# A third place for the convolution's shares, its matrices moved one transfer per step, and a reordered last unit

## The chip, the cores and the metric

The kernel runs on one core of one Trainium2 chip. The metric is the device time of one execution in microseconds. TensorE (PE) multiplies matrices, VectorE (DVE) and ScalarE (ACT) work element by element, GpSimd (POOL) issues some small transfers and SyncE (SP) issues nearly all large ones.

## What is computed

Two attention layers over x of shape (4, 256, 64, 64), float32 throughout, each as `x = x + layer(groupnorm(x))`:

```
# layer 0: queries 1x1, keys and values by a strided 2x2 convolution, 8 heads of 32 channels
q = einsum('oc,bchw->bohw', Wq, x)            # 4096 queries per image
k = conv(x, Wk, stride 2); v = conv(x, Wv, stride 2)      # 1024 keys per image
attn = softmax((q.k + q.(rel_h + rel_w)) * 32**-0.5); out = attn.v
# layer 1: qkv 1x1, attention inside 4 areas of 1024 tokens, a 7x7 depthwise convolution of v, 1x1 projection
out = softmax(q.k * 32**-0.5).v               # per area
out = out + dwconv7x7(v_full, w_pe) + b_pe
return conv1x1(out, w_proj) + b_proj
```

## The kernel before

**Units and steps.** A block is one layer on one image: `BLOCKS` holds layer 0 ("A") of the four images, then layer 1 ("B") of the four. A block has 16 units, so there are 128 units; a unit is a chunk of 512 queries of four heads. A unit has eight steps, one for each 128 keys. In a step PE makes the scores of the step (`scores`, L263), ACT takes their exponentials (L267), and PE multiplies those of the step before with the values (`weighted`, L274). DVE adds the eight pairs of exponential tiles of a unit to one pair (`sum_up`, L813); when the sum is done, `divisors` (L283) multiplies it with ones, so that each row holds the sum of its exponentials, and `divide` (L287) divides by it. To divide, the sums go through DRAM into a narrow shape, `reciprocals` inverts them (L306), they come back spread over the rows (L308, L310), and `multiply` (L313) writes the result. The last unit of all does not take this way: its sums are copied by ACT (L292), inverted in full width by DVE (L295) and multiplied (L296).

**Order.** The order on every engine is the program's own (`manual_schedule`). `at(g, j, f)` plans f for step j of unit g (a larger j runs on into the following units). `task(parts, f)` puts matrix work that is not attention into a queue `side`, of which one part is done per step, two when more than 7 parts wait and three when more than 14 wait, one less in step 2; `soon_tasks` puts tasks in at the head of the queue. In a step the order is: scores, the functions that `soon` planned for it, `weighted`, the functions of `at`, then parts of the side queue. SP issues its transfers in program order too; it waits at one whose data or buffer is not ready, and all that follow wait behind it.

**PSUM.** `ps_pair` (three buffers of two banks) holds scores, divisors and, outside the 128 units, side products; `ps_side` (one buffer of one bank) holds side products within them.

**The depthwise convolution** of layer 1 is done by PE. `plan_values` computes the values of a chunk and stores them to DRAM (`vala`, L688, and `vals`, L696), after loading the chunk `hv` of the layer's input (L665). `plan_zeros` builds in DRAM, for each of 32 groups of eight channels, a band matrix of the 7x7 taps: `matrices(k)` loads eight shifted pieces into a tile `made` (L643) and stores it as `mats[k]` (L650). A *share* is one such group of one image: `load_share` (L713) brings its matrix (`band`, L728, one transfer) and its value rows (`rows`, L731, four transfers). Both have two buffers. `convolve` (L739) is a task of two parts, one share each: after the matrix products of a share (L747) it calls `load_share(False)` for the next one not yet loaded, which takes the buffers that this share gives back. `plan_conv` plans the 16 tasks of an image; before the first of them it fills the buffers:

```
        for _ in range(2 if n == 0 else 0):
            at(0, when - 8, lambda: len(loaded) < 2 and load_share(True))
        at(0, when, lambda: task(2, convolve, b, n))
```

They start at units 36, 58, 75.5 and 93.5 and are planned 1.36, 1.06, 1.1 and 1.1 units apart. The result goes through `cout` (L758, L759) to DRAM. `load_rest` (L551) fetches it for a chunk as `cv`, `add_conv` (L573) adds attention and bias, `project` (two tasks per chunk, L157 for the products, L588 for bias and residual) makes the output, and L591 stores it.

**Layer 0's weights.** `wk0_sb` and `wv0_sb` are two constant tiles of 8 KB per partition; `make_k` and `make_v` of layer 0 (L359, L380) read them, for the last image near unit 46.

**The end.** After unit 127: the last two DVE additions, `divisors`, `divide`, `multiply` of unit 126, `add_conv` and `project` of chunk 7, then `sum_last` (L773) with the sums for a check of their size (L857 to L862), whose count each engine loads at the very end.

Of the kernel before, what the change touches and what calls it, by code (L numbers as in the profile page):

```python
# [9 lines left out]
FP = mybir.dt.float32  # L10
I32 = mybir.dt.int32
AF = mybir.ActivationFunctionType
ALU = mybir.AluOpType
AX = mybir.AxisListType

P = 128
# [39 lines left out]
def direct_path(  # L56
# [52 lines left out]
    for c in range(NCH):  # L109
        nc.sync.dma_start(first[c], xv[0][:, :, c * CH : (c + 1) * CH])  # L110
    wq0_sb = const.tile([P, CT, C], FP, name="wq0_sb")
    wk0_sb = const.tile([P, CT, 4, C], FP, name="wk0_sb")
    wv0_sb = const.tile([P, CT, 4, C], FP, name="wv0_sb")
    wqkv_sb = const.tile([P, CT, 3, C], FP, name="wqkv_sb")
    wp_sb = const.tile([P, CT, C], FP, name="wp_sb")
    nc.sync.dma_start(wk0_sb, wk0.rearrange("(t p) k o -> p t k o", p=P))
# [42 lines left out]
    def ps_pair(name):  # L159
        return psum.tile([P, 2, CH], FP, tag="s", name=name, bufs=3)  # L160
# [9 lines left out]
    def at(g, j, f):  # L170
        g, j = g + int(j // NKT), int(j % NKT)
        plan.setdefault((g, j), []).append(f)
# [103 lines left out]
                rhs=p[h // 2][:, h % 2, :], start=(j == 0), stop=(j == NKT - 1),  # L276
            )

    def divisors(g, p):

        dens[g] = ps_pair("den")[:, 0, :]
        for h in range(4):
            T.matmul(  # L283
                dens[g][HD * h : HD * h + HD, :], lhsT=ones, rhs=p[h // 2][:, h % 2, :], start=True, stop=True,
            )

    def divide(g, unit):  # L287

        den_sb = pool.tile([P, CH], FP, tag="den", name="den_sb", bufs=1)
        few = pool.tile([P, 2, CH // HD], FP, tag="few", name="few", bufs=2)  # L290
        rows = dram.tile([4, CH], FP, tag="rows", name=f"rows_{g}", bufs=4)
        S.copy(den_sb, dens.pop(g))  # L292
        if g == len(units) - 1:
            rb = pool.tile([P, CH], FP, tag="p", name="rb", bufs=10)
            V.reciprocal(rb, den_sb)  # L295
            V.tensor_mul(unit[4]()[:, unit[0], :], avs.pop(g), rb)  # L296
            spare.extend((den_sb, rb))
            return
        G.dma_start(rows, den_sb[0:P:HD, :])  # L299
        G.dma_start(few[:, 0, :], rows.rearrange("h (q n) -> (h q) n", n=CH // HD))  # L300
        made = {}

        def reciprocals():
            rb = made["rb"] = pool.tile([P, CH], FP, tag="rb", name="rb", bufs=1)
            recs = dram.tile([4, CH], FP, tag="recs", name=f"recs_{g}", bufs=4)
            V.reciprocal(few[:, 1, :], few[:, 0, :])  # L306
            V.tensor_reduce(sums[:, :, g], few, AX.X, ALU.add)  # L307
            G.dma_start(recs.rearrange("h (q n) -> (h q) n", n=CH // HD), few[:, 1, :])  # L308
            for h in range(4):
                G.dma_start(rb[HD * h : HD * h + HD, :], recs[h : h + 1, :].to_broadcast([HD, CH]))  # L310

        def multiply():
            V.tensor_mul(unit[4]()[:, unit[0], :], avs.pop(g), made["rb"])  # L313

        at(g + 1, 7, reciprocals)
        at(g + 2, 4, multiply)

    def att_of(key):
        if key not in atts:
# [146 lines left out]
    def plan_b(b, u):  # L466
# [84 lines left out]
        def load_rest(c):  # L551
            cv = chunk_tile(f"cv_{b}_{c}")
            for y in range(c * RC, (c + 1) * RC):
                n, r = y // TY, TY - 1 - y % TY
                for t in range(CT):
                    nc.sync.dma_start(  # L556
                        cv[:, t, :].rearrange("p (f r x) -> p r f x", f=TX, r=RC)[:, y - c * RC],
                        conv[b][t * P : (t + 1) * P, r * TX : (r + 1) * TX, n, :],
                    )
            if c == NCH - 1:  # L560
                load_residual(c)
            rest[c] = cv
# [1 line left out]
        def by_column(a):  # L564
            return a.rearrange("p (f q) -> p q f", f=TX)

        def add_conv(c):
            cv, att = rest[c], atts["B", b, c]
            if c < NCH - 1:
                load_residual(c)  # L570
            for t in range(CT):

                V.scalar_tensor_tensor(  # L573
                    by_column(cv[:, t, :]), by_column(cv[:, t, :]), bpe_sb[:, t : t + 1],
                    att[:, t, :].rearrange("p (q f) -> p q f", f=TX), ALU.add, ALU.add,
                )

        def project(c, to):
# [10 lines left out]
            if to == 1:  # L589
                rest.pop(c)  # L590
                nc.sync.dma_start(ov[b][:, :, c * CH : (c + 1) * CH], made_x.pop(c))  # L591

        for c in range(NCH):
            g, j = u + 2 * c + 3, 5
            at(*((g - 1, 5) if b < B - 1 or c < NCH - 1 else (g - 2, 2)), lambda c=c: load_rest(c))
            at(g, j, lambda c=c: add_conv(c))
            at(g, j + 2, lambda c=c: soon_tasks([(2, project, c, to) for to in range(CT)]))
        return [
# [15 lines left out]
    def plan_zeros(g):  # L614


        def zeros():
            width = vals[0][0].rearrange("f c x -> (f c x)").shape[0] // P
            zero = pool.tile([P, max(3 * width, BY * BX * C // P)], FP, tag="rows", name="zero", bufs=2)
            V.memset(zero, 0.0)  # L620
            flat = bands.rearrange("k y x c -> (k y x c)").rearrange("(p n) -> p n", p=P)
            nc.sync.dma_start(flat, zero[:, : flat.shape[1]])
            for b in range(B):
                for lo, hi in ((0, HALO), (HALO + HH, HH + 2 * HALO)):
                    nc.sync.dma_start(
                        vals[b][lo:hi].rearrange("r f c x -> (r f c x)").rearrange("(p n) -> p n", p=P),
                        zero[:, : (hi - lo) * width],
                    )

        def taps():  # L630
            tap = pool.tile([NTAP, C], FP, tag="cout", name="tap", bufs=2)
            nc.sync.dma_start(tap, wpe.rearrange("c k -> k c"))
            for n in range(7):
                nc.sync.dma_start(
                    bands[:, TY - 1 : TY + 6, TX + 5 - n, :].rearrange("k y c -> y k c"),
                    tap[n : n + 43 : 7, :].rearrange("y (k c) -> y k c", c=TC),
                )

        def matrices(k):
            band = pool.tile([NP, 2, TY, TX * TC], FP, tag="band", name=f"made_{k}", bufs=2)  # L640
            for dc in range(TX + 6):
                p = NP // 2 * (dc // 2 % 2) + dc % 2
                nc.sync.dma_start(  # L643
                    band[p : p + 2 * (TY + 6) - 1 : 2, dc // 4],
                    bass.AP(
                        tensor=bands.tensor, offset=bands.offset + (k * BY * BX + TX + 5 - dc) * TC,
                        ap=[[BX * TC, TY + 6], [BX * TC, TY], [1, TX * TC]],
                    ),
                )
            nc.sync.dma_start(mats[k], band)  # L650

        at(g, 0, zeros)
        at(g, 4, taps)
        for k in range(C // TC):
            at(g + 1, 6 * k, lambda k=k: matrices(k))

    stored = {}

# [54 lines left out]
    def load_share(must):  # L713

        if not shares:
            return
        b, k = shares[0]
        for c in range(NCH):
            if must:
                need(stored, (b, c))  # L720
            elif (b, c) not in stored:
                return
        shares.popleft()
        row, size = C * XT, TC * XT
        band = pool.tile([NP, 2, TY, TX * TC], FP, tag="band", name=f"band_{b}_{k}", bufs=2)
        xs = pool.tile([NP, 2, NY, TC, XT], FP, tag="rows", name=f"rows_{b}_{k}", bufs=2)
        loaded[b, k] = band, xs
        nc.sync.dma_start(band, mats[k])  # L728
        for a in range(4):
            p = NP // 2 * (a % 2)  # L730
            nc.sync.dma_start(  # L731
                xs[p : p + NP // 2, a // 2].rearrange("p y c x -> p y (c x)")[:, :, : size - 3],
                bass.AP(
                    tensor=vals[b].tensor, offset=vals[b].offset + k * size + a,
                    ap=[[row, NP // 2], [TY * TX * row, NY], [1, size - 3]],
                ),
            )
# [26 lines left out]

    def plan_conv(b, n, start):
        when = int(start * NKT)
        for _ in range(2 if n == 0 else 0):
            at(0, when - 8, lambda: len(loaded) < 2 and load_share(True))
        at(0, when, lambda: task(2, convolve, b, n))

    def sum_last():
        for n in range(2):
            V.tensor_reduce(sums[:, n, len(units) - 1 :], spare[n], AX.X, ALU.add)  # L773

    at(len(BLOCKS) * UNITS + 1, 6, sum_last)
    units = []
    for i, (layer, b) in enumerate(BLOCKS):
        u = i * UNITS
# [29 lines left out]

    def sum_up(g, j, ps):

        for i in range(2):
            if j:
                soon(1, lambda i=i: V.tensor_add(ps[0][i], ps[0][i], ps[j][i]))  # L813
        if j == NKT - 1:
            soon(3, lambda: divisors(g, ps[0]))
            soon(3, lambda: divide(g, units[g]))
# [643 lines left out]
```

## Time and profile before

| | us |
|---|---|
| median of three runs | 3265.79 (3263.93 to 3267.28) |
| the profiled execution, its own time | 3265.73 |
| its span, first to last instruction | 3264.0 |
| PE busy | 3181.3 |
| DVE, ACT busy | 2508.4, 2524.3 |
| mean granted clock of PE | 0.989 |
| moved by DMA | 421.5 MB |

"Busy" of PE counts matrix instructions from start to modelled end, so a slow clock counts as busy. "L747" is line 747 of the kernel. In a line of the order of work the columns are start, duration (both us), engine and line, operation, names of output and inputs, count; in brackets the idle time of the engine before it and what ended that. "SPq" is the queue of SP. A wait is put down to what came last.

### The profile page before, as it was taken

The page shows a single profiled execution, that of the slowest core. Times are in us where ns is not written, and L with a number is a line of the kernel's source. Part 1 is how long each engine was busy: PE and PEld are TensorE (multiplying, and loading weights), DVE is VectorE, ACT ScalarE, POOL GpSimd, SP SyncE. Part 2 cuts the span into 40 slices and gives each one's busy share as a digit, 9 for nine tenths or more (in the row PEclk, how much of TensorE's full clock was granted, in tenths as well). Part 3 has the DMA queues.
Part 4 walks back from the last instruction along what each step waited for, and adds up shares of the span by engine and source line. Part 5 has one row for each costly group of instructions (what it writes and reads, how often), then busy time and mean ns, then how long its engine had stood idle before and what let it go on. Part 6 is the DMA issues. An engine that isn't in the chain of part 4 may idle for free.

```text
span 3264.0 us, 75650 instructions
## 1 busy us (share of the span) xinstructions
PE 3181.3 (97%) x30754; PEld 963.2 (30%) x30754; DVE 2508.4 (77%) x2717; ACT 2524.3 (77%) x2993; POOL 493.6 (15%) x923
## 2 busy tenths in 40 slices
PE   7999999999999999999999899999999999999997
PEld 4233322233233333223222223232232333222221
DVE  3777896778877777778767577777787788788887
ACT  3888787787887778888867677777777777788775
POOL 0111121111211111111111111111111111111111
PEclk9999999999999999999999999999999999999998
DMA  5243434454444456677766666666554655523212
GB/s 179 44 109 78 109 89 93 96 125 108 114 114 132 122 153 154 173 174 174 187 168 151 164 155 165 174 154 170 135 156 124 156 157 152 135 68 81 65 47 57
DMA packets 648172, 421.50 MB, mean 129 GB/s; under 512 B 411756, under 2 KB 556620, under 8 KB 647816
## 3 DMA queue, kind: packets, MB, share of 16 engines
q1 hardware_dynamic: 619368, 380.11, 46.0%
q0 software_dynamic: 28448, 36.48, 4.6%
q8 instruction: 244, 4.00, 0.5%
q14 instruction: 112, 0.92, 0.1%
HBM read 318.32 MB, written 98.09 MB: 128 GB/s over the span
## 4 chain that ended last, share of the span: by engine, by line
PE 87%; DMA 6%; issue 2%; SPq 2%; DVE 1%; ACT 1%; POOL 0%; DVEq 0%; ACTq 0%; POOLq 0%
PE s L263 31%; PE av L274 27%; PE den L283 4%; DMA rows<-vals 4%; PE ops L157 3%; PE k0ps L157 3%; PE q0ps L157 3%; PE v0ps L157 3%; PE k1ps L157 3%; PE vals_ps L157 3%; PE conv_ps L747 3%; PE q1ps L157 3%; DVE p L813 1%; ACT p L267 1%; SPq L556 1%
## 5 line engine op out<-in xcount | busy, mean ns | idle before, releaser
L813 DVE TENSOR_TENSOR p<-p 128x1024 f32<-128x1024 f32 x1792 | 2111.2, 1220 | 543.6 <-ACT p L267 491.1
L267 ACT ACTIVATE p<-s 128x1024 f32<-128x1024 f32 x2048 | 2016.3, 1026 | 539.0 <-PE s L263 524.3
L263 PE MATMUL s<-q,k_A 32*128 32x512 f32 x4096 | 603.9, 640 | 6.9 <-ACT p L267 6.6
L263 PE MATMUL s<-q,k_B 32*128 32x512 f32 x4096 | 600.1, 646 | 0.3 <-ACT p L267 0.3
L274 PE MATMUL av<-p,v_B 128*32 128x512 f32 x4096 | 550.5, 608 | 0.0
L274 PE MATMUL av<-p,v_A 128*32 128x512 f32 x4096 | 549.7, 604 | 0.0
L310 POOL DMA_DIRECT2D rb<-recs x508 | 252.0, 501 | 451.5 <-DMA recs<-few 367.1
L263 PEld LDWEIGHTS s<-q,k_B 32*128 32x128 f32 x4096 | 166.3, 184 | 386.7 <-issue 297.0
L263 PEld LDWEIGHTS s<-q,k_A 32*128 32x128 f32 x4096 | 173.2, 183 | 338.0 <-issue 253.5
L308 POOL DMA_DIRECT2D recs<-few x127 | 70.0, 551 | 1284.8 <-DVE sums L307 1207.5
L274 PEld LDWEIGHTS av<-p,v_B 128*32 128x32 f32 x4096 | 87.9, 108 | 384.2 <-issue 340.5
L274 PEld LDWEIGHTS av<-p,v_A 128*32 128x32 f32 x4096 | 88.6, 108 | 381.3 <-issue 333.5
L747 PE MATMUL conv_ps<-rows,band 88*32 88x128 f32 x4096 | 139.2, 277 | 28.9 <-DMA rows<-vals 28.9
L747 PEld LDWEIGHTS conv_ps<-rows,band 88*32 88x32 f32 x4096 | 123.8, 139 | 100.6 <-issue 80.3
L157 PE MATMUL ops<-cv,wp_sb 128*32 128x512 f32 x1024 | 136.3, 612 | 9.9 <-issue 6.4
L300 POOL DMA_DIRECT2D few<-rows x127 | 72.3, 569 | 477.5 <-DMA rows<-den_sb 468.0
L283 PE MATMUL den<-p,ones 128*32 128x512 f32 x1024 | 138.7, 604 | 2.2 <-DVE p L813 2.2
L299 POOL DMA_DIRECT2D rows<-den_sb x127 | 74.4, 586 | 436.7 <-ACT den_sb L292 429.9
L157 PE MATMUL k0ps<-taps,wk_sb 128*32 128x256 f32 x2048 | 128.9, 383 | 3.0 <-ACT taps L245 3.0
L157 PE MATMUL q1ps<-h,wqkv_sb 128*32 128x512 f32 x1024 | 131.5, 592 | 0.0
L157 PE MATMUL vals_ps<-hv,wqkv_sb 128*32 128x512 f32 x1024 | 130.2, 594 | 0.0
L157 PE MATMUL k1ps<-h,wqkv_sb 128*32 128x512 f32 x1024 | 128.7, 592 | 0.2 <-ACT cout L758 0.2
(86 smaller groups left out, 1690.8 us busy)
## 6 DMA issues: line engine op xcount, KB each, us to landing
rows<-vals SPq DMA_DIRECT2D x512, 195.9 KB
rb<-recs POOLq DMA_DIRECT2D x508, 64.0 KB, 3.2
band<-mats SPq DMA_DIRECT2D x128, 176.0 KB
vala<-vout SPq DMA_DIRECT2D x128, 144.0 KB
vals<-vout SPq DMA_DIRECT2D x128, 144.0 KB
vc<-vala SPq DMA_DIRECT2D x64, 288.0 KB
hq<-in_x SPq DMA_DIRECT2D x32, 512.0 KB
xc<-in_x SPq DMA_DIRECT2D x32, 512.0 KB
```

The costliest lines, as they stand in the source:

```text
L157: T.matmul(out[cols, :], lhsT=lhsT[:, cols], rhs=rhs, start=start, stop=stop)
L263: T.matmul(pairs[h // 2][:, h % 2, :], lhsT=k[rows, unit[0], j * P : (j + 1) * P], rhs=q[rows, :], start=True, stop=True,)
L267: exps = [lambda i=i: S.activation(p[i], pairs[i], AF.Exp, scale=SCALE) for i in range(2)]
L274: T.matmul(av[HD * h : HD * h + HD, :], lhsT=v[:, j, unit[0] * P + HD * h : unit[0] * P + HD * h + HD], rhs=p[h // 2][:, h % 2, :], start= ...
L283: T.matmul(dens[g][HD * h : HD * h + HD, :], lhsT=ones, rhs=p[h // 2][:, h % 2, :], start=True, stop=True,)
L299: G.dma_start(rows, den_sb[0:P:HD, :])
L300: G.dma_start(few[:, 0, :], rows.rearrange("h (q n) -> (h q) n", n=CH // HD))
L308: G.dma_start(recs.rearrange("h (q n) -> (h q) n", n=CH // HD), few[:, 1, :])
L310: G.dma_start(rb[HD * h : HD * h + HD, :], recs[h : h + 1, :].to_broadcast([HD, CH]))
L556: nc.sync.dma_start(cv[:, t, :].rearrange("p (f r x) -> p r f x", f=TX, r=RC)[:, y - c * RC], conv[b][t * P : (t + 1) * P, r * TX : (r + 1 ...
L747: T.matmul(ps[HD * m : HD * m + HD, (2 * k + i) * size : (2 * k + i + 1) * size].rearrange("p (y x) -> p y x", y=NY), lhsT=band[:, half].r ...
L813: soon(1, lambda i=i: V.tensor_add(ps[0][i], ps[0][i], ps[j][i]))
```

## The change

It has four edits. (1) The two weight tiles of layer 0 become one tile of 16 KB, and from image 1 on every third share has its matrix and rows in that place; so three shares are loaded instead of two. (2) The nine transfers of a matrix are planned one per step (the store in the eighth step, with the last load), eight steps to a matrix instead of six. (3) The last unit's sum takes seven of eight tiles; its eighth is multiplied with ones by PE and accumulated. Its reciprocal reads PSUM without the copy. (4) The last chunk's addition and projection are written out half by half, in the order in which the two halves of its attention come; `reciprocals` and `multiply` of unit 126 are planned earlier; the output of the chunk leaves in two transfers.

```diff
-    wk0_sb = const.tile([P, CT, 4, C], FP, name="wk0_sb")
-    wv0_sb = const.tile([P, CT, 4, C], FP, name="wv0_sb")
+    wkv = const.tile([P, 2, CT, 4, C], FP, tag="wkv", name="wkv")
+    wk0_sb, wv0_sb = wkv[:, 0], wkv[:, 1]
...
-    def divisors(g, p):
+    def divisors(g, *ps):
         dens[g] = ps_pair("den")[:, 0, :]
+        for n, p in enumerate(ps):
+            for h in range(4):
+                T.matmul(... ones, rhs=p[h // 2][:, h % 2, :], start=(n == 0), stop=(n == len(ps) - 1))
...
     def divide(g, unit):
+        if g == len(units) - 1:
+            rb = pool.tile([P, CH], FP, tag="p", name="rb", bufs=10)
+            V.reciprocal(rb, dens[g])
+            V.tensor_mul(unit[4]()[:, unit[0], :], avs.pop(g), rb)
+            spare.extend((dens.pop(g), rb))
+            return
...
-        at(g + 1, 7, reciprocals)
-        at(g + 2, 4, multiply)
+        at(g + 1, 7 if g < len(units) - 2 else 4, reciprocals)
+        at(g + 2, 4 if g < len(units) - 2 else 0, multiply)
...
+        def project_last(c):
+            cv, xm, ps = rest[c], made_x[c], [ps_pair("ops")[:, 0, :] for _ in range(CT)]
+            for t in range(CT):
+                if t == CT - 1:
+                    divide(len(units) - 1, units[-1])
+                    add_conv(c, [t])
+                    for n in range(2):
+                        V.tensor_reduce(sums[:, n, len(units) - 1 :], spare[n], AX.X, ALU.add)
+                for to in range(CT):
+                    product(ps[to], lhsT=wp_sb[:, t, to * P : (to + 1) * P], rhs=cv[:, t, :],
+                        start=(t == 0), stop=(t == CT - 1))
+            for to in range(CT):
+                x_to = xm[:, to, :].rearrange("p (q f) -> p q f", f=TX)
+                V.scalar_tensor_tensor(x_to, by_column(ps[to]), bproj_sb[:, to : to + 1], x_to, ALU.add, ALU.add)
+                nc.sync.dma_start(ov[b][:, to, c * CH : (c + 1) * CH], xm[:, to, :])
...
+            if b == B - 1 and c == NCH - 1:
+                at(g - 2, 2, lambda c=c: load_rest(c))
+                at(g - 1, 1, lambda c=c: add_conv(c, [0]))
+                at(g - 1, 3, lambda c=c: project_last(c))
+                continue
...
         for k in range(C // TC):
-            at(g + 1, 6 * k, lambda k=k: matrices(k))
+            for n in range(TX + 6):
+                at(g + 1, 8 * k + n, lambda k=k, n=n: matrices(k, [n]))
...
-        band = pool.tile([NP, 2, TY, TX * TC], FP, tag="band", name=f"band_{b}_{k}", bufs=2)
-        xs = pool.tile([NP, 2, NY, TC, XT], FP, tag="rows", name=f"rows_{b}_{k}", bufs=2)
+        if b and (b * (C // TC) + k) % 3 == 2:
+            place = const.tile([P, 2 * CT * 4 * C], FP, tag="wkv", name=f"share_{b}_{k}")
+            n = 2 * NY * size
+            xs = place[:NP, :n].rearrange("p (h y c x) -> p h y c x", h=2, y=NY, c=TC)
+            band = place[:NP, n : n + 2 * TY * TX * TC].rearrange("p (h y m) -> p h y m", h=2, y=TY)
+        else:
+            band = pool.tile(... tag="band", bufs=2)
+            xs = pool.tile(... tag="rows", bufs=2)
...
-        for _ in range(2 if n == 0 else 0):
-            at(0, when - 8, lambda: len(loaded) < 2 and load_share(True))
+        room = 3 if b else 2
+        for _ in range(room if n == 0 else 0):
+            at(0, when - 8, lambda: len(loaded) < room and load_share(True))
...
     def sum_up(g, j, ps):
+        if j == NKT - 1 and g == len(units) - 1:
+            soon(2, lambda: divisors(g, ps[0], ps[j]))
+            return
```

`sum_last` and its place in the plan are gone; its two reductions stand in `project_last`.

More of the change, by code (lines that the diff above doesn't have):

```diff
@@ L277, in weighted @@
             )
-    def divisors(g, p):
+    def divisors(g, *ps):
         dens[g] = ps_pair("den")[:, 0, :]
[L282 to L285, printed above, removed]
-    def divide(g, unit):
+        for n, p in enumerate(ps):
+            for h in range(4):
+                T.matmul(
+                    dens[g][HD * h : HD * h + HD, :], lhsT=ones, rhs=p[h // 2][:, h % 2, :],
+                    start=(n == 0), stop=(n == len(ps) - 1),
+                )
+    def divide(g, unit):
+        if g == len(units) - 1:
[4 more added lines that the diff above has]
+            return
         den_sb = pool.tile([P, CH], FP, tag="den", name="den_sb", bufs=1)
@@ L292, in divide @@
         S.copy(den_sb, dens.pop(g))
[L293 to L298, printed above, removed]
         G.dma_start(rows, den_sb[0:P:HD, :])
@@ L565, in by_column, with add_conv @@
             return a.rearrange("p (f q) -> p q f", f=TX)
-        def add_conv(c):
+        def add_conv(c, ts=range(CT)):
             cv, att = rest[c], atts["B", b, c]
@@ L570, in add_conv @@
                 load_residual(c)
-            for t in range(CT):
+            for t in ts:
                 V.scalar_tensor_tensor(
@@ L591, in project @@
                 nc.sync.dma_start(ov[b][:, :, c * CH : (c + 1) * CH], made_x.pop(c))
+        def project_last(c):
[7 more added lines that the diff above has]
+                for to in range(CT):
+                    product(
+                        ps[to], lhsT=wp_sb[:, t, to * P : (to + 1) * P], rhs=cv[:, t, :],
+                        start=(t == 0), stop=(t == CT - 1),
+                    )
+            for to in range(CT):
+                x_to = xm[:, to, :].rearrange("p (q f) -> p q f", f=TX)
+                V.scalar_tensor_tensor(x_to, by_column(ps[to]), bproj_sb[:, to : to + 1], x_to, ALU.add, ALU.add)
+                nc.sync.dma_start(ov[b][:, to, c * CH : (c + 1) * CH], xm[:, to, :])
         for c in range(NCH):
             g, j = u + 2 * c + 3, 5
-            at(*((g - 1, 5) if b < B - 1 or c < NCH - 1 else (g - 2, 2)), lambda c=c: load_rest(c))
+            if b == B - 1 and c == NCH - 1:
[3 more added lines that the diff above has]
+                continue
+            at(g - 1, 5, lambda c=c: load_rest(c))
             at(g, j, lambda c=c: add_conv(c))
@@ L637, in taps, with matrices @@
                 )
-        def matrices(k):
-            band = pool.tile([NP, 2, TY, TX * TC], FP, tag="band", name=f"made_{k}", bufs=2)
-            for dc in range(TX + 6):
+        made = {}
+        def matrices(k, dcs):
+            if k not in made:
+                made[k] = pool.tile([NP, 2, TY, TX * TC], FP, tag="band", name=f"made_{k}", bufs=2)
+            band = made[k]
+            for dc in dcs:
                 p = NP // 2 * (dc // 2 % 2) + dc % 2
@@ L649, in matrices @@
                 )
-            nc.sync.dma_start(mats[k], band)
+            if TX + 5 in dcs:
+                nc.sync.dma_start(mats[k], made.pop(k))
         at(g, 0, zeros)
@@ L724, in load_share @@
         row, size = C * XT, TC * XT
-        band = pool.tile([NP, 2, TY, TX * TC], FP, tag="band", name=f"band_{b}_{k}", bufs=2)
-        xs = pool.tile([NP, 2, NY, TC, XT], FP, tag="rows", name=f"rows_{b}_{k}", bufs=2)
+        if b and (b * (C // TC) + k) % 3 == 2:
[4 more added lines that the diff above has]
+        else:
+            band = pool.tile([NP, 2, TY, TX * TC], FP, tag="band", name=f"band_{b}_{k}", bufs=2)
+            xs = pool.tile([NP, 2, NY, TC, XT], FP, tag="rows", name=f"rows_{b}_{k}", bufs=2)
         loaded[b, k] = band, xs
@@ L766, in plan_conv @@
         when = int(start * NKT)
-        for _ in range(2 if n == 0 else 0):
-            at(0, when - 8, lambda: len(loaded) < 2 and load_share(True))
+        room = 3 if b else 2
+        for _ in range(room if n == 0 else 0):
+            at(0, when - 8, lambda: len(loaded) < room and load_share(True))
         at(0, when, lambda: task(2, convolve, b, n))
[L771 to L775, printed above, removed]
     units = []
```

## Prediction

> **What bounds the kernel now.** I read the busy table first, then the waits of PE, then the granted clock in slices of 10 us, then the order of instructions around the longest waits, then SP's own queue.
>
> ```profile
> PE 3181.3 (97%) x30754; PEld 963.2 (30%) x30754; DVE 2508.4 (77%) x2717; ACT 2524.3 (77%) x2993; POOL 493.6 (15%) x923
> PE conv_ps L747 <- DMA rows<-vals: 28.9, 19, 7.0
> PE gm_A L222 <- DVE mv_A L217: 16.3, 1, 16.3
> PE s L263 <- ACT p L267: 6.9, 4, 5.8
> PE ops L157 <- issue: 6.4, 1, 6.4
> ```
>
> TensorE is the bound: it is idle for 3264.0 - 3181.3 = 82.7 us, and DVE and ACT have 23% to spare. The columns of a wait are total us, times, longest. The largest item is the convolution waiting for its input rows: 28.9 us, every case after 1520 us, that is in batches 1 to 3; batch 0 has none. 16.3 us is the first load, which the change does not touch. The 5.8 us at 568.6 us is one wait, the 6.4 us is the end.
>
> A wait also costs clock. The columns of the next line are the stretch, its length, busy time of PE, PEld, DVE, ACT and POOL with counts, granted clock, DMA share and GB/s; below it is the order of work there, without the other engines' lines.
>
> ```profile
> 1850.00:1860.00 10.00, 5.11 (x48) 1.99 (x48) 1.07 (x3) 0.88 (x1) 2.53 (x5) 0.53 0.89 234
> 1843.86 1.06 PE L747 MATMUL conv_ps<-rows,band 88*32 88x128 f32 x32
> ...
> 1846.72 1.75 SPq L731 DMA_DIRECT2D rows<-vals  x4
> ...
> 1851.10 3.94 SPq L731 DMA_DIRECT2D rows<-vals  x4
> ...
> 1854.02 0.67 PE L747 MATMUL conv_ps<-rows,band 88*32 88x128 f32 x8 [7.04 <-DMA rows<-vals]
> 1855.55 1.52 PE L747 MATMUL conv_ps<-rows,band 88*32 88x128 f32 x24 [0.86 <-DMA rows<-vals]
> 1857.00 2.09 PE L263 MATMUL s<-q,k_B 32*128 32x512 f32 x8
> ```
>
> A share's rows are issued at 1846.7 and needed at 1847.0, so PE stands until 1855.6; then the s group takes 2.09 us where it takes 1.14 when warm. Adding such excesses after the six clusters of waits (1649, 1854, 2112, 2268, 2469, 2769 us) gives 2.7 + 2.7 + 1.7 + 3.2 + 3.2 + 1.6 = 15.1 us. **The whole price of late shares is 28.9 + 15.1 = 44 us.**
>
> SP's queue at the 5.8 us wait, and the end:
>
> ```profile
> 541.75 10.45 SPq L643 DMA_DIRECT2D made<-bands  x8
> 553.97 0.32 SPq L650 DMA_DIRECT2D mats<-made  x1
> 554.40 1.12 SPq L688 DMA_DIRECT2D vala<-vout  x2
> ...
> 559.99 1.20 SPq L665 DMA_DIRECT2D hv<-xmid  x1
> 3238.97 3.35 DVE L295 RECIPROCAL rb<-den_sb 128x512 f32<-128x512 f32 x1 [1.11 <-ACT den_sb L292]
> ...
> 3244.35 2.10 DVE L573 SCALAR_TENSOR_TENSOR cv<-cv,bpe_sb,att_B 128x512 f32<-128x512 f32 x2
> ...
> 3245.57 5.84 PE L157 MATMUL ops<-cv,wp_sb 128*32 128x512 f32 x32 [6.40 <-issue]
> ```
>
> One matrix's burst holds SP from 541.8 to 554.3; ACT then waits 6.6 us for hv (landed 566.8) and PE for ACT's exponentials. At the end DVE works alone while PE waits, and PE then runs 32 cold matmuls.
>
> **What the Trainium skill says.** "TensorE: Matmul & The Clock Gate", part 1, says that about 3.4 us of idleness halves the clock and that a similar busy time restores it. The trace agrees in direction (0.53 granted, 2.09 against 1.14 us), but here 1.69 us (at 2112) was already enough for an s group of 1.82. "DMA: Bandwidth & Descriptors", rules for kernel authors, says to issue early and wait late: the shares that were waited for took 8.8 us (1846.7 to 1855.6) to 11 us (1851.1 to 1862.6) from issue to use, while two tasks in a row stand 3 us apart. The same page, on the anatomy of a DMA, says that a DMA's semaphore wait happens on the issuing sequencer: SP waits 358.3 us for conv_ps (L728), so what stands behind a share stands with it.
>
> **Part 1, the third share.** Instructions, bytes and the slots at which SP loads are the same; each slot now loads the share after the one it loaded before. Share i arrives when share i-1 did. Before, share i-1 made PE wait w and share i is needed d later; now w is gone and share i waits w - d if that is positive. d is 1.0 us when two parts follow in one step (1649) and 3.1 us otherwise (1.06 conv, 1.0 s, 1.0 av). So: 1649: w 2.0, d 1.0, left 1.0, taken as 1.4 because of the half that lands later; 1854: w about 8.5 to the second half's landing, d 3.1, left 5.4 and its 2.7 cold; the others have w of at most 1.7 and leave nothing. Left: 9.5 us. **Gain 44 - 9.5 = 34.5 us**; bounds 15 (see the first rival) and 44. The weights' merged tile could make the first k product wait for both weight loads; DMA moved 342 GB/s in the first 21.3 us, 7.3 MB, more than the 6.3 MB up to wv, and k starts at 21.2: nothing, at most 3 us if that cover is gone. The weights' last use is near unit 46 and the first share in their place near unit 56, so that wait is nothing.
>
> **Part 2, matrices.** 256 loads at 0.78 us and 32 stores at 0.32 us stay; they go from nine together every six steps to one per step (two every eighth), and end at unit 35 instead of 27. Between 541 and 560 us are about four steps, so SP issues 4 or 5 before hv and not 9 with a 1.8 us wait for the landing: hv comes 4 x 0.78 + 1.8 = 4.9 us earlier or more. That takes most of 5.8 us and of the cold after it (about 2.5), and the 1.1 us at 717 and 723 us: 9.4 at most; I take 8. Against it: between 725 and 945 us SP, now issuing 41 us in 100, gets ten more matrices of 8 x 0.78 + 0.32 + 1.5 = 8 us, 33 in 100 more. Queued behind are hq, xs, xa, vala, vals, xmid, hv; ACT and then PE wait for them. The loads are planned five steps (15 us) before use, so one late by a store's wait is covered; I charge 2. **Gain 6 us**, bounds -10 (one 8.3 us stall and a little) and +9.4.
>
> **Part 3, the end.** Before, the last add ends at 3237.2 and the last product's DVE step at 3252.2; after that come 11.8 us that stay (check of sums, load of the count, drains). After: the reciprocals of the last unit but one move ahead (0.44 us on DVE), so the sixth add ends at 3234.9; two adds (2.35) are dropped and 8 PE records added (1.0), den is done at 3236.9 and the ACT copy (0.58) gone. DVE: multiply 0.68, xm of chunk 6 0.75, half of cv 1.06, reciprocal 3.35 (now from PSUM, unseen; taken as the SBUF one), multiply 0.69, other half 1.06: 3242.5, then two reductions 1.34 that only PE's work covers. If a PSUM pair is free, PE does the first half of the product early, then 16 cold matmuls (2.9) and chunk 6's last eight (1.5), which now stand behind the new task in PE's order: with its DVE step 3247.6, a gain of 4.6. But den, chunk 6 and two outputs are four pairs and the pool has three: if the second output waits until den's reduction (3243.1), 24 cold matmuls, 4.4, follow, and the gain is 2.3. **I take 3 us**; bounds 0 (rb late for the moved multiply: it lands near 3234, 1 us of slack) and 6 (PE stays warm). Two stores of 256 KB instead of one end within the 11.8 us.
>
> **Sum.** 34.5 + 6 + 3 = 43.5 us off 3265.73 (span 3264.0 plus 1.7 around it): 3222. The median of the runs, 3265.79, is the same within 0.1.
>
> **Rivals.** (1) SP, not the buffer, is late. Around 2000 us it issues 69 us in 100, and slot 1846.4 came after a 2.9 us hv issue. If PE running ahead only meets the same queue sooner, about half of part 1 returns as waits: 3265.7 - 17 - 6 - 3 = 3240. For it: four of the six clusters lie where SP is over 55%. Against: one slot is as much lead as the wait lacked. (2) The shares still come together with the need, because release or order makes the third place useless: parts 2 and 3 only, 3257. Against: the place is apart from the pool and its last reader is long done. (3) Slower: the ten matrices moved to 725-945 us. If their stores' waits hold the block inputs behind them, each such case costs what 568 us cost, 8.3; from six of them the gain of 45 (without my 2) is used up; nine give 3265.7 - 45 + 75 = 3296. For it: SP goes to 74 in 100 there. Against: PE has no wait at all between 725 and 900, with 175.0 busy of 175.0, and SP was at 65 around 650 with burst and all.
>
> **Numbers.** 0.2% (6.5 us) is about what a measurement of this kernel can tell from no change. Forecast 3222, own range 3211 to 3233: 60%. Rival 1: 20%. Rival 2: 7%. Rival 3: 9%. A mixture that ends within 0.2%: 4%. Faster 0.87, same 0.04, slower 0.09. The range takes in the forecast with its bounds and rival 1: 3206 to 3248.
>
> **What would show it.** Right: the waits of conv_ps for rows fall from 28.9 to under 8 us, idle PE from 83 to about 47, no slice at 568 us below full clock, the last DVE product step 11 to 12 us before the end with one reciprocal of 3.4 us ahead of it. Wrong: waits for rows above 15 us (rival 1), unchanged (2), or new waits of PE for ACT or DVE between 725 and 945 us (3).

## The result, and the profile after

The changed kernel takes 3215.48 us (median of four runs, 3211.28 to 3217.78) where the kernel before takes 3264.86 (four runs, 3263.58 to 3267.28). The ratio on record is 0.9842 (95% interval 0.983 to 0.9854); the two medians alone give 0.9849. The profiled execution took 3214.37 us with a span of 3212.4, against 3265.73 and 3264.0: 51.6 us of span. Forecast were 3222 us, 43.5 less.

The busy line of the page of the changed kernel:

```profile
PE 3161.1 (98%) x30762; PEld 960.6 (30%) x30762; DVE 2505.4 (78%) x2715; ACT 2523.5 (79%) x2992; POOL 490.0 (15%) x923
```

PE is idle for 3212.4 - 3161.1 = 51.3 us instead of 82.7, and its busy time is 20.2 us less with eight more matrix records: the granted clock rose with it, from a mean of 0.989 to 0.996, so most of that is slow clock that went.

What PE waited for in the changed kernel (total us, times, longest):

```profile
PE gm_A L223 <- DVE mv_A L218: 16.2, 1, 16.2
PE conv_ps L787 <- DMA share<-vals: 5.6, 2, 4.1
PE ops L158 <- DVE sums L605: 4.4, 1, 4.4
PE ops L158 <- DVE xm L592: 4.1, 3, 2.7
...
PE conv_ps L787 <- DMA rows<-vals: 0.7, 1, 0.7
```

The convolution waits 6.3 us for its shares instead of 28.9; the 5.8 us wait for ACT is gone; a new item of 4.4 us stands at the end.

**Where the time came from.** The copy of a unit's finished attention sums (`av_sb`, once per unit, L834 before, L873 after) is a clock that both kernels share. Its time before minus its time after, unit by unit (copies counted from 1), moves only at a few places:

| number of the copy | gained there, us | what stood there before |
|---|---|---|
| 19 | 0.5 | a longer scores group at 509 us (2.32 against 1.83), no wait listed |
| 21 | 9.2 | the wait for hv at 568 us |
| 27 | 1.3 | the waits at 717 and 723 us |
| 60 | 0.8 | a late share at 1524 us |
| 65, 72 | 9.5, 4.4 | late shares at 1649 and 1854 us |
| 80 and 82 | 0.7 + 3.6 | 2056 and 2112 us |
| 88, 96, 108 | 7.6, 7.2, 5.7 | 2268, 2469 and 2769 us |
| after the last copy | 2.0 | the end (30.5 us became 28.5) |

By sections, net of small moves: 11.0 up to copy 28, 39.2 from copy 56 to 108, 2.0 at the end. These are single executions: the same end of the program takes 27.3 to 30.0 us in five other traces that have it (28.5 here), the old end 29.7 to 30.9 in four.

The cluster of 1854 us, in the order of work of the changed kernel (start, duration; in brackets the wait):

```profile
1823.49 1.06 PE L787 MATMUL conv_ps<-rows,band 88*32 88x128 f32 x32
...
1825.71 1.85 SPq L771 DMA_DIRECT2D share<-vals  x4
...
1826.43 1.06 PE L787 MATMUL conv_ps<-rows,band 88*32 88x128 f32 x32
...
1833.69 0.67 PE L787 MATMUL conv_ps<-share 88*32 88x128 f32 x8 [4.14 <-DMA share<-vals]
...
1835.78 1.52 PE L787 MATMUL conv_ps<-share 88*32 88x128 f32 x24 [1.42 <-DMA share<-vals]
...
1837.22 2.09 PE L264 MATMUL s<-q,k_B 32*128 32x512 f32 x8
```

The first share of the next task, on which PE stood before, is there at 1826.4. The second one is issued at 1825.7, in the slot that brought the first one before, lands near 1835.8 and is needed at 1829.5: 5.6 us of waits, where the prediction worked out 5.4. In the four other executions with three loaded shares and the tasks at the end of the queue, the waits for shares are 5.0 to 8.1 us in all, so that the agreement within 0.2 us is partly luck.

SP's queue ahead of the hv load:

```profile
541.16 2.52 SPq L675 DMA_DIRECT2D made<-bands  x2
543.80 1.88 SPq L722 DMA_DIRECT2D vala<-vout  x2
...
551.49 0.84 SPq L675 DMA_DIRECT2D made<-bands  x1
552.77 0.34 SPq L699 DMA_DIRECT2D hv<-xmid  x1
```

Three matrix transfers stand between 541 and 553 us, where the kernel before had nine transfers and a wait; hv is issued at 552.8 instead of 560.0.

The end:

```profile
3187.47 3.34 DVE L295 RECIPROCAL rb<-den 128x512 f32<-128x512 f32 x1
3192.61 0.67 DVE L605 TENSOR_REDUCE sums<-den 128x1 f32<-128x512 f32 x1
3193.43 6.22 PE L158 MATMUL ops<-cv,wp_sb 128*32 128x512 f32 x32 [4.44 <-DVE sums L605]
3199.72 0.75 DVE L592 SCALAR_TENSOR_TENSOR xm<-ops,bproj_sb,xm 128x512 f32<-128x512 f32 x1
```

PE waits for the reduction of den, not for cv, and then has 32 records ahead of it, most of them cold. The reciprocal costs the same from PSUM (3.34) as from SBUF (3.35). The last product step on DVE is that of chunk 6 (L592).

### The profile page after: what moved, and what is told of

Its sections match the earlier page's. It is cut to its first block, busy times and chain, and to the rows that moved or that the text cites. A ratio compares the mean times of both kernels' runs of the same rounds, so it can differ in the third digit from the quotient of the medians.

```text
span 3212.4 us, 75608 instructions
## 1 busy us (share of the span) xinstructions
PE 3161.1 (98%) x30762; PEld 960.6 (30%) x30762; DVE 2505.4 (78%) x2715; ACT 2523.5 (79%) x2992; POOL 490.0 (15%) x923
## 5 line engine op out<-in xcount | busy, mean ns | idle before, releaser
L158 PE MATMUL k0ps<-taps,wkv 128*32 128x256 f32 x2048 | 128.9, 383 | 3.0 <-ACT taps L246 3.0
L158 PE MATMUL q0ps<-hq,wq_sb 128*32 128x512 f32 x1024 | 128.2, 592 | 0.0
L158 PE MATMUL v0ps<-wkv,taps 128*32 128x256 f32 x2048 | 126.1, 379 | 0.3 <-ACT v_A L396 0.3
```

Source lines behind the costliest of these rows:

```text
L158: T.matmul(out[cols, :], lhsT=lhsT[:, cols], rhs=rhs, start=start, stop=stop)
```

## The experiments

Ratios are to the kernel before on the same chip, where it took 3269 to 3273 us at the median (three chips). "Gain by unit copies" is read from the copies as above, against the profiled execution of the kernel before.

**The third share alone.** The kernel before with

```diff
+    wkv = const.tile([P, 2, CT, 4, C], FP, tag="wkv", name="wkv")
+    wk0_sb, wv0_sb = wkv[:, 0], wkv[:, 1]
...
+        if b and (b * (C // TC) + k) % 3 == 2:
+            place = const.tile([P, 2 * CT * 4 * C], FP, tag="wkv", name=f"share_{b}_{k}")
...
+        room = 3 if b else 2
```

> The kernel before with the third share's place alone (edit 1). The unit times of the changed kernel, set against those of the kernel before, put 39 us of the gain into the units in which batches 1 to 3 are convolved. If the third share alone does this, this kernel takes about 3226 us (39 less), its waits of conv_ps for rows or share are about 6 us, and the wait at 568 us stays. If the gain there needs the spread matrices or the changed end as well, it is above 3240.

Measured: 3231.67 us, ratio 0.9864 (0.9843 to 0.9884). The medians differ by 40.0 us. Gain by unit copies between 56 and 108: 37.8 us; waits for rows and share 6.7 us; the wait of 6.1 us at 570 us is there. The third place alone brings the middle part.

**The matrices alone.** The kernel before with

```diff
-            at(g + 1, 6 * k, lambda k=k: matrices(k))
+            for n in range(TX + 6):
+                at(g + 1, 8 * k + n, lambda k=k, n=n: matrices(k, [n]))
```

> The kernel before with the matrices' transfers one per step alone (edit 2). By the unit times it brings 11 us, all before unit 28: about 3254 us, no wait at 568 us, the 28.9 us of conv_ps unchanged. If new waits between 725 and 945 us ate part of it, less than 8 us are gained.

Measured: 3260.7 us, ratio 0.9951 (0.9934 to 0.9967), that is 11 to 22 us. Gain by unit copies up to unit 28: 11.0 us, in the same two places as in the changed kernel (9.2 at copy 21, 1.3 at 27). Waits for rows: 30.2 us. Between copies 31 and 34 it lost 3.2 us, with two short waits of PE for DVE's sums, of which the longer is

```profile
832.10 1.67 PE L283 MATMUL den<-p,ones 128*32 128x512 f32 x6 [0.85 <-DVE p L819]
```

Between copies 64 and 79 this execution lost 7.6 us again, of which 4.9 came back by 108; the shares' waits lie there, and the matrices are all made by unit 35. The ratio says 16 us, the two medians 10.9 and the copies 11.0 up to copy 28; why the ratio says more is left open.

**The end alone.** The kernel before with edits 3 and 4 (`divisors` over two tiles, `project_last`, the earlier plan of unit 126).

> The kernel before with the end alone (edits 3 and 4). The changed kernel is 2.0 us nearer to its end after the last unit than the kernel before: about 3263 us, within the noise, and in the trace 2 us less from the last copy of the attention sums to the end. If the end were worth what a free PSUM pair would give, it would be 4.6 us.

Measured: 3269.12 us, ratio 0.999 (0.9979 to 1.0001): no difference that can be told. In the trace the stretch from the last copy to the end is 29.1 us instead of 30.5. The three parts together, 37.8 + 11.0 + 1.4 = 50.2 us, make up the 51.6 but for 1.4 us: no interaction larger than the spread of these readings shows.

**Three places, but two shares loaded.** The changed kernel with

```diff
-        room = 3 if b else 2
+        room = 2
...
-        if not shares:
+        if not shares or len(loaded) > 1:
             return
```

> The changed kernel, with the third place but never more than two shares loaded: the place rotates, so a load finds its buffer free one share earlier, but it stands at the same point of SP's order as in the kernel before. Theory of the prediction (what counts is that each slot loads the next share but one, the order): all clusters come back, about 3254 us. Rival (what counts is that SP no longer waits for the products of the share before it loads): none comes back, 3215 us. A mixture: in the kernel before SP waited for the buffer by 4 to 11 us just ahead of the clusters at 2112, 2268, 2469 and 2769 us, but by at most 1.6 us at 1649 and 1854 us, where its own queue was late. Then only these two come back, 13 us: about 3228 us.

Measured: 3253.45 us, ratio 0.9936 (0.9916 to 0.9957). Gain by unit copies from 56 to 108: 9.1 us instead of 39.2. The mixture was wrong: the waits of five of the six clusters are back, and the one at 2769 us has 1.6 of its 3.4 us again. The theory of order is close. What PE waited for:

```profile
PE conv_ps L787 <- DMA rows<-vals: 18.4, 8, 4.4
PE conv_ps L787 <- DMA share<-vals: 9.1, 5, 2.6
```

What SP's queue waited for, in the kernel before (two lines), here (two lines) and in the changed kernel (one):

```profile
SPq L728 <- PE conv_ps L747: 358.3, 46, 23.8
SPq L759 <- ACT cout L758: 73.0, 35, 5.6
...
SPq L799 <- ACT cout L798: 239.2, 45, 15.5
SPq L768 <- PE conv_ps L787: 144.3, 11, 23.8
...
SPq L768 <- PE conv_ps L787: 343.7, 40, 24.1
```

SP's wait for the buffer fell from 358 to 144 us, but the wait for `cout` rose from 73 to 239. The order of work at the cluster of 2469 us shows why:

```profile
2452.27 1.06 PE L787 MATMUL conv_ps<-rows,band 88*32 88x128 f32 x32
2453.40 0.59 ACT L798 COPY cout<-conv_ps 128x512 f32<-128x512 f32 x1
2454.01 0.38 SPq L799 DMA_DIRECT2D conv<-cout  x1
2454.49 0.39 SPq L768 DMA_DIRECT2D share<-mats  x1
...
2460.92 0.46 PE L787 MATMUL conv_ps<-share 88*32 88x128 f32 x8 [2.58 <-DMA share<-vals]
```

The store of the task's result stands ahead of the load in SP's order and needs the same matrix products. The wait that was taken away is there under another name, and a free buffer alone brings 9.1 us. In the changed kernel, where the clusters are gone, SP still waits 344 us for the products: what the third place brings is not the end of that wait, but loads one share ahead.

**The kernel before, tasks at the head of the queue.** Two places, one line:

```diff
-        at(0, when, lambda: task(2, convolve, b, n))
+        at(0, when, lambda: soon_tasks([(2, convolve, b, n)]))
```

> The kernel before with one line changed: a convolution task goes to the head of the side queue (soon_tasks) and not to its end, so that tasks come at their planned distance of 8 to 9 steps and not, as at 1649 and 1854 us, two or three within 12 us. Two places, no other edit. Theory (a share is late because tasks come in bunches, and the third place buys the lead that the bunches need): the 28.9 us of conv_ps fall under 6 us and the kernel takes about 39 us less, 3226 us where the kernel before takes 3265. Rival (SP's queue is late by itself, whatever the distance): more than 15 us of waits for rows stay and less than 20 us are gained.

Measured: 3224.39 us, ratio 0.9852 (0.9835 to 0.9868). PE has no wait for rows at all any more. Gain by unit copies from 56 to 108: 41.7 us. In the kernel before the first parts of three tasks in a row start at 1605.7, 1635.8 and 1649.1 us:

```profile
1605.66 1.06 PE L747 MATMUL conv_ps<-rows,band 88*32 88x128 f32 x32
...
1635.84 1.06 PE L747 MATMUL conv_ps<-rows,band 88*32 88x128 f32 x32
...
1649.09 0.46 PE L747 MATMUL conv_ps<-rows,band 88*32 88x128 f32 x8 [0.47 <-DMA rows<-vals]
```

The same stretch here:

```profile
1623.04 1.06 PE L747 MATMUL conv_ps<-rows,band 88*32 88x128 f32 x32
1625.98 1.06 PE L747 MATMUL conv_ps<-rows,band 88*32 88x128 f32 x32
1647.33 1.93 PE L747 MATMUL conv_ps<-rows,band 88*32 88x128 f32 x64
1673.34 1.06 PE L747 MATMUL conv_ps<-rows,band 88*32 88x128 f32 x32
```

The tasks stand 24 and 26 us apart, and two places are enough. **The late shares came from bunched tasks; the third place covers for the bunches.** The ratio of this one line, 0.9852, can't be told from that of all four edits, 0.9842. It also brings a new wait, for an hv, that costs 7.2 us by the copies:

```profile
2021.04 2.07 PE L263 MATMUL s<-q,k_B 32*128 32x512 f32 x4 [3.35 <-ACT p L267]
```

**The changed kernel, tasks at the head.** The same line in the changed kernel.

> The changed kernel with convolution tasks at the head of the side queue. If bunches cause what is left, the wait of 5.6 us for a share at 1834 us and its cold matmuls (2.7 us) go: about 8 us less than the changed kernel, 3207 us. If other tasks, now put off by up to two parts, become late, it is not faster than the changed kernel.

Measured: 3214.06 us, ratio 0.9815 (0.9798 to 0.9832). The waits for shares are gone, but a new one came. What stands around it (the engine lines of ACT and PE only):

```profile
2008.77 0.81 ACT L246 ACTIVATE hv<-hv,norm_B 128x512 f32<-128x512 f32 x1 [5.42 <-DMA hv<-xmid]
...
2010.55 2.08 PE L264 MATMUL s<-q,k_B 32*128 32x512 f32 x4 [3.33 <-ACT p L268]
```

SP issued hv at 1999.0, behind the loads of two shares, and ACT used it 9.8 us later. By the copies, the 8.3 us that the last cluster still cost (copy 72) are gained, and 7.2 are lost again at this wait (copy 79). The ratios of 0.9815 and 0.9842 have intervals that overlap at the edge, so the run times don't show that this kernel is faster.

**The second output in the side bank.** The changed kernel with

```diff
-            cv, xm, ps = rest[c], made_x[c], [ps_pair("ops")[:, 0, :] for _ in range(CT)]
+            cv, xm = rest[c], made_x[c]
+            ps = [ps_pair("ops")[:, 0, :], psum.tile([P, CH], FP, tag="side", name="ops_side", bufs=1)]
```

> The changed kernel with the second output of project_last in the side bank of PSUM instead of a fourth pair. If the 4.4 us that PE stands at the end is the wait for den's pair (released by the reduction of den), the first half of both products is done ahead of the reciprocal, 16 cold records instead of 32 are left after it, and the last DVE step comes about 2.3 us sooner after the last copy of the attention sums. If the wait is for cv's second half anyway, nothing moves.

Measured: one run, 3220.68 us; its time says nothing on 2 us, the trace does. From the last copy to the end it is 25.7 us instead of 28.5.

```profile
3198.90 1.26 PE L158 MATMUL ops_side<-cv,wp_sb 128*32 128x512 f32 x8
...
3203.12 1.06 PE L158 MATMUL ops<-cv,wp_sb 128*32 128x512 f32 x8 [2.96 <-DVE cv L577]
...
3204.01 1.04 PE L158 MATMUL ops_side<-cv,wp_sb 128*32 128x512 f32 x8
```

PE now waits for cv, with the first halves done. So the 4.4 us were the wait for den's pair, as the prediction had it. 2.8 us came of it, not 2.3. Here eight records after the wait take 1.04 us, which is the warm time. That is not certain: in the first version below, with the same end, the next groups of eight take 1.79 and 1.95 us, and the stretch is 26.0 us.

**Bursts every eight steps.** The changed kernel with

```diff
-            for n in range(TX + 6):
-                at(g + 1, 8 * k + n, lambda k=k, n=n: matrices(k, [n]))
+            at(g + 1, 8 * k, lambda k=k: matrices(k, range(TX + 6)))
```

> The changed kernel with a matrix's nine transfers together again, but every eight steps instead of six. hv loads are planned at steps 6 modulo 8, so each now stands six steps behind a burst, where in the kernel before the one at 560 us stood two steps behind it. Theory (it is a burst just ahead of a load that is needed soon): no wait of PE above 2 us between 500 and 950 us, unit times as in the changed kernel within 3 us. Rival (nine transfers in a row cost wherever they stand): waits of several us come back there, up to the 11 us of the kernel before.

Measured: one run, 3219.36 us. Between 500 and 950 us PE's only wait is one of 0.3 us, and the gain by unit copies up to 28 is 10.4 us:

```profile
713.24 1.93 PE L158 MATMUL v0ps<-wkv,taps 128*32 128x256 f32 x32 [0.29 <-ACT v_A L396]
```

Nine transfers in a row cost nothing that shows when they stand six steps ahead of hv, so it was not the length of the burst that cost 11 us. That it was its place, two steps ahead of hv, is likely; bursts are also rarer here, and this one execution can't tell the two apart.

**The changed kernel again, and two versions beside it on one chip.**

> The changed kernel once more, as the measure on the same chip for the two that run beside it: 0.984 of the kernel before.

Measured: 3217.07 us, ratio 0.9847 (0.9831 to 0.9862), with 5.0 us of waits for shares. Between copies 31 and 34 this execution loses 2.3 us, which the first one of the same kernel did not.

The first version has the head of the queue, the side bank, and in `plan_values`

```diff
-        at(0, when, load)
+        at(0, when - 3, load)
```

> The changed kernel with convolution tasks at the head of the side queue, the second output of project_last in the side bank, and the loads of hv planned three steps earlier, since with tasks at the head PE stood 3.3 us at 2010 us for an hv that SP issued behind two shares. Expected against the changed kernel: 5.6 us of waits and 2.7 of cold at 1834 us, 0.7 at 1639 us and 3 us at the end, 12 us together less, a ratio to the kernel before near 0.980. If the earlier hv takes chunk buffers that others need, new waits of ACT or DVE for chunks appear and less than 6 us are gained.

Measured: 3201.2 us, ratio 0.9791 (0.9776 to 0.9806): faster than both kernels. Some of its waits of PE:

```profile
PE k0ps L158 <- ACT taps L246: 3.0, 1, 3.0
PE ops L158 <- DVE cv L577: 3.0, 1, 3.0
...
PE ops L158 <- DVE xm L592: 1.4, 2, 0.7
```

Between 500 and 3090 us no wait is above 0.4 us, and the one for hv near 2010 us is gone. Against the changed kernel beside it, (0.9847 - 0.9791) x 3268.9 = 18 us (16 by the medians); by the copies 12.0 of them lie between copies 56 and 108, and the end is 26.0 us instead of 27.3.

The second version has the head of the queue and the side bank, without the third place:

> The changed kernel with convolution tasks at the head of the side queue and the second output in the side bank, but without the third place: the shares have their two places again. If the distance of the tasks, not the number of places, decides, no wait for rows above 2 us comes back and it is within 5 us of the kernel with tasks at the head and three places (0.9815 of the kernel before). If both are needed for the whole gain, it is above 0.985.

Measured: 3210.01 us, ratio 0.9817 (0.9798 to 0.9836). No wait for rows in the list. Once the tasks keep their distance, the third place is worth nothing that these runs can measure: by the copies from 56 to 108 the gain is 44.2 us with two places and 43.3 with three. The ratios, 0.9817 and 0.9815, are not quite alike to compare, since the kernel with two places has the side bank as well (2.8 us).

## Why the prediction was right

**Part 1 (34.5 forecast, 39.2 by the copies).** The mechanism held in its detail: same slots, each one share ahead, and what is left is w - d. Left were 5.6 us at 1834 (forecast 5.4) and 0.7 at 1639 (forecast 1.4), nothing elsewhere. The kernel with three places and two loads shows that the place without the order brings little. Mis-sized was the whole price of late shares. In the kernels with the tasks at the head, where no share is late, the clusters give back 48.9 us by the copies, not 44; what is left in the changed kernel costs 9.2, against 9.5 forecast. The term that is short is "cold matmuls": 15.1 us were counted from the groups next to the waits, and each of the six clusters cost 0.2 to 1.2 us more than its idle time plus those groups (at 2268 us 7.6 against 6.9, at 1854 us 12.7 against 12.0). One reading was wrong without effect: other waits than those at 1649 and 1854 us were called at most 1.7 us, but a share at 2277 us waited 2.1, and one at 1655 us 3.4 and 1.3.

**Part 2 (6 forecast, 11.0 by the copies).** The step "hv comes 4.9 us earlier or more" was right (7.2). The stall at 568 us cost 9.2 us with its slow clock, not 8.3, and all of it went; 0.5 at copy 19 was not forecast. The charge of 2 us for new waits between 725 and 945 us looks needless in the profiled execution, where PE is busy 219.86 of the 220 us. But it was fair: all seven other traces here in which the matrices move one per step lose 1.8 to 3.2 us between copies 31 and 34, near 830 to 880 us, and none of the traces with bursts does. That the profiled execution did not lose them is luck; as a rule part 2 brings about 9 us. Why they are lost was not followed up. A slip without effect: ten matrices of 8 us in 220 us are 36 in 100 more for SP, not 33.

**Part 3 (3 forecast, 2.0).** The 3 us lay between two branches, 4.6 with a free pair and 2.3 without, and the second came. Four pairs for three buffers and den's reduction as the release came as worked out: moved by the 49.63 us between the two last copies, PE starts at 3243.1, the time forecast. The 32 records behind it (the 24 of the forecast and chunk 6's eight) took 6.22 us instead of 4.4 + 1.5. That PE stood 4.4 us ahead of them was not in the forecast, and its likeness to the 4.4 us of 24 cold records is chance. The side bank shows the other branch: with a free bank the stretch is another 2.8 us shorter. How cold the 32 records are differs (5.07 us in the changed kernel again, 6.43 with two loads), and the run times show none of this part.

**The sum.** 34.5 + 6 + 3 = 43.5 against 39.2 + 11.0 + 2.0 = 52.2, less small moves, 51.6. Of the difference, 4.7 us are part 1's slow clock after waits, which the sum counted too short; 5.0 are part 2, of which 2 are a charge that this execution escaped and others did not; 1.0 goes the other way at the end.

**The rivals.** Rival 1 (SP itself is late) fell: the waits for shares went from 28.9 to 6.3 us. Rival 2 fell with the same number. Rival 3 fell in size: no stall like that of 568 us came, but the 2 us at 830 to 880 us lie where it looked. But the prediction took the bunched tasks as given; that the kernel before reaches the same gain in the middle with one line and two places shows that a deeper cause stood one step further back than the forecast looked.

**The skill's places.** The advice of the Trainium skill's "DMA: Bandwidth & Descriptors", rules for kernel authors, to issue early and wait late held; here early meant one share earlier in the order of the queue. That a transfer's wait is the issuer's wait (same page, on the anatomy of a DMA) held as well: SP's waits for the products are 358 us before and 344 after. The kernel with three places and two loads adds that taking one wait out of an ordered queue helps little, 9.1 us of 39.2, when the next one in it waits for the same products.

## What to carry to other kernels

When a double-buffered load is late, look first at the distances of its uses: uneven uses need more buffers than their mean distance does, and putting them back at their distance can replace a buffer, as it did here. In a queue that issues in order, ask of each wait what the instruction behind it waits for, and of each long burst what stands behind it that is due soon. Price a stall of a nearly full TensorE with its slow clock: by the copies, 1.9 to 4.1 us on top of 1.7 to 9.3 us of idleness here. Read a small gain in more than one trace: one execution showed 2 us too much in part 2.

## What the runs showed of the hardware that was not expected

A wait of 1.69 us in the kernel before (at 2112 us) was followed by slow matrix groups: the eight score records after it took 1.82 us, where they take 1.14 when warm, and the granted clock from 2113 to 2116 us was 0.57. After two waits of 0.30 and 1.30 us, close together just before 2270 us, they took 2.09. The Trainium skill's "TensorE: Matmul & The Clock Gate", part 1, gives about 3.4 us of idleness for that. The length of the gap alone does not decide either: with three places and two loads a wait of 1.97 us at 2101 us was followed by groups of 1.14 us, and in the side-bank kernel one of 2.96 us by groups of 1.06 and 1.04. What decides is not shown by these traces.

The reciprocal of 128x512 took 3.34 us from PSUM and 3.35 from SBUF.

The kernel before took 3264.86 us at the median when the result was measured, and 3268.88, 3271.62 and 3273.45 on three chips later; on one of these chips alone its 23 runs lie between 3264.60 and 3285.21. So only ratios on one chip, or unit copies in the trace, could tell 10 us.
